# Layer 3 of a four-layer kernel: the first term of y written by VectorE, the first pair's sums beside the second's, stores on ScalarE's queue, and a new step plan

## The chip, the core and the metric

The kernel runs on one NeuronCore of a Trainium2 chip. The core has a matrix engine (TensorE, PE in the profile), VectorE (DVE), ScalarE (ACT), GpSimd (POOL), and a sync engine (SP) that here only issues DMAs. The engines run in parallel, each through its own instructions in order, and wait for one another by semaphores. A PE matmul writes to PSUM, eight banks of 128 x 512 fp32; VectorE and ScalarE read and write PSUM and SBUF; GpSimd works on SBUF. The metric is the device time of one launch in microseconds (us), the median of some runs.

## The reference

A chain of four layers on x of shape (2, 128, 64, 64), fp32. The change is in layer 3, a small Mamba over the channels of each pixel: the 128 channels are 8 tokens of 16 features.

```python
def _mamba(seq, ...):                       # seq: (B*H*W, 8, 16)
    xz = seq @ in_proj_w.T
    xi, z = jnp.split(xz, 2, axis=-1)       # 32 each
    xs = silu(causal depthwise conv of 4 taps over the tokens (xi))
    dt, Bm, Cm = split(xs @ x_proj_w.T)     # 1, 16, 16
    dt = softplus(dt @ dt_proj_w.T + dt_proj_b)
    dA = jnp.exp(dt[..., None] * A)
    dBx = dt[..., None] * Bm[:, :, None, :] * xs[..., None]
    def step(h, inp):
        dA_t, dBx_t, C_t = inp
        h = dA_t * h + dBx_t
        return (h, jnp.einsum('nds,ns->nd', h, C_t))
    ...                                     # scan over the 8 tokens
    y = ys + xs * D
    y = y * silu(z)
    return y @ out_proj_w.T
...
# layer 3: x + silu(groupnorm(mamba(x)))    (4 groups of 32 channels, per image)
```

With h_t = dA_t * h_(t-1) + dBx_t, the sum over states of C_t * h_t falls into two: the sum of C_t * dBx_t, which is (sum over n of B_n * C_n) * dt * xs, and the sum of C_t * dA_t * h_(t-1). The kernel computes the first by itself; it is "the first term of y".

## The kernel before

Layer 3 works on 16 chunks: 2 images x 8 chunks of 512 pixels (`Chunk3`). The channels of a chunk lie on the 128 partitions and the pixels in the free dimension. After the projections, a tile of [128, 2, 512] holds the 8 tokens x 32 inner channels: two halves `i` of four strips of 32 partitions. The scan over 8 tokens is made in four steps `k` of two tokens `o` each; `PLACE[k]` names the half and the strip pair of step k: k = 0 and 1 are the two strip pairs of the first half, k = 2 and 3 those of the second. In the scan, the tiles `A` and `D` have 16 states x 32 channels as 128 partitions x 4 groups, for 512 pixels: [128, 4, 512] for each token.

For each chunk:
- `xs_` and `sz_`: PE projections of x, ScalarE's Silu. `b_`, `c_`: the rows B and C; `b_` copies B by ScalarE into `bs` and stores it to DRAM (`rows`). `dt_`, `e_exp`, `e_ln`, `dt_add`: softplus, with the last add on GpSimd; `dtx_`: dt * xs on GpSimd into `e`; `put` stores dt to DRAM (`ddt`).
- `spread` and `load` bring dt and B back by DMA, spread over the partitions of the scan (`dtr`, `D`). All these DMAs are issued by SP, in order.
- `da_`: ScalarE's Exp makes A. `rx_`: PE spreads dt * xs into PSUM, and `db_` (VectorE) multiplies D by it. `mul` (GpSimd): A = A * h_(t-1), half a token (128 x 1024) at a time. `add` (VectorE, or GpSimd for some): D = D + A, which is the new h. The products and sums of successive tokens are the recurrence; `todo` and `advance` write their order for each step.
- `pc_`: PE spreads C into PSUM (`q`, two buffers); `hc_` (VectorE): A = A * C, a unit `u` of 128 x 1024 at a time; `y_` (PE): sums over the states into a 32-partition strip of the bank `y`.
- `cb_`, `cbx_`, `ecb_`: the first term. `ecb_` writes it into the tile `dt`, half by half; `y1_` adds it to `y` by a matmul with the identity, and `y0_` begins y with D * xs by a matmul with a diagonal matrix.
- `yg_`: y times silu(z) (VectorE). `xr_`: output projection, ScalarE's copy into x. `bn_`: statistics for the group norm. When an image's chunks are done, class `Norm` finishes it: `silu` on ScalarE, `load` of the kept x, `store`: an add on VectorE or GpSimd and the DMA out.

The loop `for s` runs over all (chunk, step) pairs as a pipeline written out by hand. In iteration s, step s-1 is read out (`hc_`, `y_`: `pc_` in the loop), step s does its recurrence (`cc`), step s+1 gets its `db_` and `da_` (`nc_`), and step s+2 its loads (`n2`). Each iteration has four groups `g`; the dictionaries `first` and `extra` hang further work at (k, g), ahead of and behind the group's own, for the chunk in work, the one before (`old`) and the next two (`fut`, `fut2`). Everything is under `tc.manual_schedule()`: each engine runs its instructions in the order of this program.

Lines of the profile: `one` L1165 (PE for `xs_`, `sz_`, `dt_`, `cbx_`), `bc_` L1184, store of `rows` L1193, `cb_` L1200, `dt_add` L1217, `dtx_` L1220, `put` L1224, `spread` L1232, `load` L1244, `ecb_` L1251, `rx_` L1261, `db_` L1265, `da_` L1271, `mul` L1278, `add` L1283, `pc_` L1295, `hc_` L1300, `y0_` L1304, `y1_` L1308, `y_` L1316, `yg_` L1321, `xr_` L1326. PSUM holds one bank each for `misc` and `y`, two for `rx`, and two pairs for `q`. Each call of a matmul on fp32 appears as two records.

Of the kernel before, what the change touches and what calls it, by code (L numbers as in the profile page):

```python
# [7 lines left out]
F32 = mybir.dt.float32  # L8
# [49 lines left out]
def conv_seq_kernel(ctx: ExitStack, tc: tile.TileContext, a: dict, out: bass.AP):  # L58
# [1031 lines left out]
    with ExitStack() as c3:  # L1090
# [61 lines left out]
        class Chunk3:  # L1152
# [4 lines left out]
            def __init__(self, b, ci):  # L1157
                self.b, self.ci = b, ci
                self.sl = slice(ci * T, (ci + 1) * T)
                self.A, self.D, self.rx, self.dtr = {}, {}, {}, {}  # L1160
# [13 lines left out]
            def sz_(self, i):  # L1174
                if i == 0:
                    self.sz = wt("sz", bufs=3)
# [11 lines left out]
            def b_(self):  # L1188
                p = self.bc_(0)
                self.bs = wt("bs", (P, T))  # L1190
                nc.scalar.copy(self.bs, p)
                self.rows = dr.tile([P, T], F32, tag="rows", name="rows")
                nc.sync.dma_start(self.rows, self.bs)  # L1193
# [4 lines left out]
            def cb_(self):  # L1198
                self.cb = wt("cb", (P, T), bufs=1)
                nc.vector.tensor_mul(self.cb, self.bs, self.pc)  # L1200

            def dt_(self, i):
                if i == 0:
                    self.e = wt("e")
                    self.dt = wt("dt")
# [16 lines left out]
            def put(self):  # L1222
                self.ddt = dr.tile([P, 2, T], F32, tag="ddt", name="ddt")
                nc.sync.dma_start(self.ddt, self.dt)  # L1224
# [25 lines left out]
            def ecb_(self, i):  # L1250
                nc.vector.tensor_mul(self.dt[:, i, :], self.e[:, i, :], self.pcb)  # L1251
# [15 lines left out]
            def da_(self, k):  # L1267
                sl = slice(1, 2) if k == 0 else slice(0, 2)
                self.A[k] = wt("A", (P, 2, 4, T), bufs=3)
                for g in range(4):  # L1270
                    act(self.A[k][:, sl, g, :], self.dtr[k][:, sl, :], AF.Exp,  # L1271
                        scale=aneg[:, 2 * NS + g : 2 * NS + g + 1])

            def mul(self, k, o, half):
                g = slice(2 * half, 2 * half + 2)
                h = (self.D[k, 0] if o else self.D[k - 1, 1])[:, g, :]
                a_ = self.A[k][:, o, g, :]
                nc.gpsimd.tensor_mul(a_, a_, h)  # L1278

            def add(self, k, o, half, eng):  # L1280
                g = slice(2 * half, 2 * half + 2)
                d = self.D[k, o][:, g, :]
                eng.tensor_add(d, d, self.A[k][:, o, g, :])  # L1283
# [14 lines left out]
            def hc_(self, k, u):  # L1298
                a_ = self.A[k][:, 1, 2 * u : 2 * u + 2, :] if k == 0 else self.A[k][:, :, u, :]
                nc.vector.tensor_mul(a_, a_, self.q.pop((k, u)))  # L1300

            def y0_(self, i):
                self.y = ps.tile([P, T], F32, tag="y", name="y")
                mm(self.y, lhsT=diag_d, rhs=self.xs[:, i, :], start=True, stop=False,  # L1304
                   skip_group_check=True)

            def y1_(self, i):
                mm(self.y, lhsT=ident, rhs=self.dt[:, i, :], start=False, stop=False,  # L1308
                   skip_group_check=True)

            def y_(self, k, u):
                i, j = PLACE[k]
                last = (1 if k == 0 else 3)
                for o, g in self.unit(k, u):
                    r = slice(32 * (j + o), 32 * (j + o) + 32)
                    mm(self.y[r], lhsT=rep[:, 0:32], rhs=self.A[k][:, o, g, :], start=False,  # L1316
# [355 lines left out]
```

## Time and profile before

| what | us |
|---|---|
| median of 3 runs | 6776.94 (6775.4 to 6785.25) |
| the profiled execution, device time | 6768.67 |
| its span, first to last instruction | 6766.5 |
| layer 3 in it | from 5617 to the end |
| one chunk of layer 3, steady | 65 |

Busy shares over the whole span: PE 88%, DVE 81%, ACT 66%, POOL 80%. They mix four layers; the stages of layer 3 must be read from its own window. In the rows below, "x224" counts instructions, the mean is in ns, and what stands behind the bar is idle time of the engine just before these instructions and what ended it. Layer 3's largest groups on each engine, from 5540 us on:

| line, engine | what | count | mean ns |
|---|---|---|---|
| L1278 POOL | product A * h | 224 | 2358 |
| L1265 DVE | D times rx | 224 | 1212 |
| L1300 DVE | A times C | 224 | 1210 |
| L1283 DVE / POOL | D + A | 128 / 64 | 1720 / 2986 |
| L1295, L1316 PE | C spread, sums into y | 896, 896 | 721, 666 |
| L1271 ACT | Exp of 128 x 1024 | 192 | 1137 |

From 5700 to 6700 us the DMAs moved 158.56 MB, 159 GB/s. By line, KB of an issue and median us to landing: D<-rows 256 KB 6.0, dtr<-ddt 64 KB 2.1, ddt<-dt 512 KB 9.3, rows<-bs 256 KB 2.1, kept<-x 2048 KB 10.9.

### The profile page before, as it was taken

What the parts mean: (1) busy time and instruction counts of PE and PEld (TensorE: products, weight loads), DVE (VectorE), ACT (ScalarE), POOL (GpSimd) and SP (SyncE); (2) the same over time, 40 slices, a digit from 0 to 9 for tenths busy, and PEclk for the clock granted to TensorE, in tenths of its full rate; (3) what the DMA queues carried; (4) which work ended last, traced back from release to release, by engine and by line L of the source; (5) the groups of instructions that cost most, each with busy time, mean ns of one, the idle gap of its engine ahead of it and who ended that gap; (6) DMA issues with size and microseconds to landing.
All of it is one profiled execution on the core that took longest, in us unless ns stands there. A gap on an engine that the chain in (4) does not pass through costs nothing. (4 is left out here: it accounts for less than half of the span.)

```text
span 6766.5 us, 66235 instructions
## 1 busy us (share of the span) xinstructions
PE 5937.2 (88%) x19980; PEld 2785.3 (41%) x19980; DVE 5486.3 (81%) x4456; ACT 4471.8 (66%) x7736; POOL 5390.1 (80%) x2471
## 2 busy tenths in 40 slices
PE   8888888888888888888889999999999997888887
PEld 2222222222222222222248877887788882222221
DVE  7999999999999999999976665665566674777677
ACT  7887788877788777887765654554555564444443
POOL 6999999999999999999976665555566665787676
PEclk7888777877788777887789999999999996898788
DMA  6556666665666656666520000000000004667565
GB/s 185 144 148 159 165 147 146 149 151 143 152 153 155 151 144 152 153 154 150 144 62 1 5 3 1 1 1 1 1 1 1 1 1 107 172 147 164 143 162 124
DMA packets 397882, 700.60 MB, mean 104 GB/s; under 512 B 73801, under 2 KB 76242, under 8 KB 396882
## 3 DMA queue, kind: packets, MB, share of 16 engines
q1 hardware_dynamic: 396640, 694.32, 42.2%
q8 instruction: 157, 2.57, 0.2%
q14 instruction: 203, 1.66, 0.1%
q10 hardware_dynamic: 882, 2.04, 0.1%
HBM read 584.80 MB, written 111.28 MB: 103 GB/s over the span
## 5 line engine op out<-in xcount | busy, mean ns | idle before, releaser
L384 POOL TENSOR_TENSOR dbu<-dus,bs 128x1024 f32<-128x1024 f32 x1024 | 2439.2, 2422 | 114.6 <-DVE h L428 97.6
L428 DVE TENSOR_TENSOR_SCAN h<-da,hst,dbu 128x1024 f32<-128x1024 f32 x896 | 2092.4, 2342 | 86.9 <-ACT dbu L412 83.0
L397 ACT ACTIVATE da<-dts,aneg 128x512 f32<-128x512 f32 (+1 forms) x2048 | 1410.0, 689 | 348.3 <-DVE h L428 310.0
L924 POOL TENSOR_TENSOR sum<-sum,sc 128x1024 f32<-128x1024 f32 x384 | 906.7, 2361 | 491.7 <-ACT sc L919 487.9
L886 ACT COPY sc<-s 128x512 f32<-128x512 f32 x1024 | 597.7, 585 | 859.5 <-PE s L881 745.7
L881 PE MATMUL s<-q,k 128*128 128x256 f32 x4096 | 1052.0, 380 | 7.1 <-DVE k L858 3.5
L893 DVE TENSOR_TENSOR mx<-mx,s 128x512 f32<-128x512 f32 x896 | 610.0, 681 | 546.0 <-ACT sc L886 544.8
L936 PE MATMUL av<-sc,v 128*128 128x256 f32 x4096 | 1049.5, 379 | 2.5 <-ACT sc L919 2.5
L451 PE MATMUL y<-hc,cst 128*32 128x512 f32 x4096 | 875.2, 753 | 192.8 <-DVE hc L440 179.2
L440 DVE TENSOR_TENSOR hc<-h,pc 128x1024 f32<-128x1024 f32 x704 | 843.2, 1198 | 9.7 <-PE y L451 8.1
L881 PEld LDWEIGHTS s<-q,k 128*128 128x128 f32 x4096 | 776.5, 190 | 140.9 <-issue 29.0
L936 PEld LDWEIGHTS av<-sc,v 128*128 128x128 f32 x4096 | 768.8, 190 | 103.2 <-ACT sc L919 3.9
L438 POOL TENSOR_TENSOR hc<-h,cs 128x1024 f32<-128x1024 f32 x320 | 764.8, 2390 | 1.2 <-issue 1.2
L1278 POOL TENSOR_TENSOR A<-A,D 128x1024 f32<-128x1024 f32 x224 | 524.1, 2358 | 230.4 <-DVE D L1283 208.2
L417 PE MATMUL pc<-xd,sel 16*128 16x512 f32 x1024 | 704.5, 778 | 1.4 <-DVE hc L440 1.3
L916 DVE TENSOR_TENSOR sc<-sc,pm 128x1024 f32<-128x1024 f32 x512 | 620.9, 1213 | 0.9 <-PE pm L912 0.9
L919 ACT ACTIVATE sc<-sc 128x1024 f32<-128x1024 f32 x512 | 541.9, 1059 | 8.6 <-DVE sc L916 8.1
L341 PE MATMUL misc<-xd,w_dt 9*128 9x512 f32 x504 | 360.5, 802 | 130.3 <-ACT x L480 69.7
L451 PEld LDWEIGHTS y<-hc,cst 128*32 128x32 f32 x4096 | 125.2, 120 | 846.4 <-DVE hc L440 417.3
L1265 DVE TENSOR_TENSOR D<-D,rx 128x1024 f32<-128x1024 f32 x224 | 269.0, 1212 | 173.0 <-PE q L1295 109.9
L412 ACT ACTIVATE dbu<-hst,dbu,df 128x1 f32<-128x1 f32 x896 | 337.7, 377 | 68.1 <-POOL dbu L384 44.9
L1271 ACT ACTIVATE A<-dtr,aneg 128x1024 f32<-128x1024 f32 (+1 forms) x256 | 245.8, 1031 | 201.5 <-PE y L1316 103.8
(262 smaller groups left out, 7714.0 us busy)
## 6 DMA issues: line engine op xcount, KB each, us to landing
dts<-ddt SPq DMA_DIRECT2D x512, 256.0 KB, 5.5
dus<-ddu SPq DMA_DIRECT2D x512, 256.0 KB, 5.1
D<-rows SPq DMA_DIRECT2D x448, 256.0 KB, 6.0
bs<-rows SPq DMA_DIRECT2D x1024, 64.0 KB, 5.0
cs<-rows SPq DMA_DIRECT2D x1024, 64.0 KB, 3.3
ddt<-dt SPq DMA_DIRECT2D x128, 256.0 KB, 2.0
ddu<-dtu SPq DMA_DIRECT2D x128, 256.0 KB, 4.1
dtr<-ddt SPq DMA_DIRECT2D x448, 64.0 KB, 2.2
```

Source lines behind the costliest of these rows:

```text
L384: nc.gpsimd.tensor_mul(t, self.dus[q], _bc(self.bs[g], 1, [P, 2, T]))
L397: act(t[:, i, sl], self.dts[q][:, i, sl], AF.Exp, scale=an[:, g, 2 * q + i : 2 * q + i + 1])
L417: mm(t, lhsT=sel[32:48, 4 * g : 4 * g + 4, :].rearrange("p n d -> p (n d)"), rhs=self.xd[32:48, :], start=True, stop=True)
L428: nc.vector.tensor_tensor_scan(ho, ai, bi, init, ALU.mult, ALU.add)
L438: nc.gpsimd.tensor_mul(t, self.h[u], _bc(self.cs[gq(u)[0]], 1, [P, 2, T]))
L440: nc.vector.tensor_mul(t, self.h[u], _bc(self.pc[u // 2], 1, [P, 2, T]))
L451: mm(self.y[q // 2][r : r + 32, :], lhsT=sum4, rhs=self.hc[u][:, i, :], start=False, stop=(u % 8 >= 6), skip_group_check=True)
L881: mm(p[:, o, :], lhsT=j.k[m // 8][:, m % 8 * P : m % 8 * P + P], rhs=self.q, start=True, stop=True)
L893: nc.vector.tensor_max(self.mx, self.s[0][:, 0:2, :] if u == 1 else self.mx, self.p[u])
L916: nc.vector.tensor_sub(s, s, _bc(self.pm[:, :], 1, [P, 4, NQ]))
L924: nc.gpsimd.tensor_add(self.sum, self.s[0] if w == 1 else self.sum, self.s[w])
L936: mm(self.av, lhsT=self.job.v[m // 8][:, m % 8, :], rhs=self.s[u // 2][:, m % 4, :], start=(m == 0), stop=(m == 31))
```

## The change

- `ecb_` no longer writes into `dt`: VectorE writes the first term straight into the PSUM bank `y`. `y1_` and its matmuls go. `y` is now one tile for all of layer 3; one matmul with `start=True` writes it once ahead of the loop, and every later matmul into it, `y0_` too, accumulates (`start=False`) on what VectorE wrote.
- The first step's sums (k = 0, one strip, four groups) are no longer made by themselves: `y_` for k = 1 sums the groups of (1, 0), (1, 1) and (0, 1) in turn, into three strips. To hold the first step's A until then it gets a tile of its own, `A0` (one buffer); `A` with its three buffers serves k = 1 to 3.
- The stores of `rows` and of `ddt` are issued by ScalarE in place of SP.
- A table `PLAN` writes out, for each step k and group g, the order of C (`hc_`), D (`db_`), products `m`, adds `v` on VectorE and `g` on GpSimd; "time" is `dt_add` and `dtx_`. It replaces `todo`, `advance` and the order in the loop's body.
- Other work changes place: `sz_` goes from two chunks ahead into the chunk's own steps 1 and 2; `xs_` goes from step 2 to step 1; `dt_` half in step 2, half in step 3; `b_` from the end of step 3 to the start of step 0 of the chunk before; `cbx_` and `ecb_` into the chunk's own steps 1 and 3. Numbers of buffers follow (`sz` 3 to 2, `bs` 2 to 1, `cb` 1 to 2, `e` 2 to 3, `dt` 2 to 1).
- x is kept in four DMAs of 1024 pixels in place of one; the group norm's loads, adds and stores are made in eight pieces of 512 pixels in place of four of 1024, and its small operations are hung elsewhere. For the second image `silu` stays at 1024.

```diff
             def b_(self):
                 p = self.bc_(0)
-                self.bs = wt("bs", (P, T))
+                self.bs = wt("bs", (P, T), bufs=1)
                 nc.scalar.copy(self.bs, p)
                 self.rows = dr.tile([P, T], F32, tag="rows", name="rows")
-                nc.sync.dma_start(self.rows, self.bs)
+                nc.scalar.dma_start(self.rows, self.bs)
...
             def put(self):
                 self.ddt = dr.tile([P, 2, T], F32, tag="ddt", name="ddt")
-                nc.sync.dma_start(self.ddt, self.dt)
+                nc.scalar.dma_start(self.ddt, self.dt)
...
             def ecb_(self, i):
-                nc.vector.tensor_mul(self.dt[:, i, :], self.e[:, i, :], self.pcb)
+                nc.vector.tensor_mul(y, self.e[:, i, :], self.pcb)
...
             def da_(self, k):
+                t = wt("A0", (P, 1, 4, T), bufs=1) if k == 0 else wt("A", (P, 2, 4, T), bufs=3)
                 sl = slice(1, 2) if k == 0 else slice(0, 2)
-                self.A[k] = wt("A", (P, 2, 4, T), bufs=3)
...
             def y0_(self, i):
-                self.y = ps.tile([P, T], F32, tag="y", name="y")
-                mm(self.y, lhsT=diag_d, rhs=self.xs[:, i, :], start=True, stop=False,
+                mm(y, lhsT=diag_d, rhs=self.xs[:, i, :], start=False, stop=False,
                    skip_group_check=True)
 
-            def y1_(self, i):
-                mm(self.y, lhsT=ident, rhs=self.dt[:, i, :], start=False, stop=False,
-                   skip_group_check=True)
-
             def y_(self, k, u):
-                i, j = PLACE[k]
-                last = (1 if k == 0 else 3)
-                for o, g in self.unit(k, u):
-                    r = slice(32 * (j + o), 32 * (j + o) + 32)
-                    mm(self.y[r], lhsT=rep[:, 0:32], rhs=self.A[k][:, o, g, :], start=False,
-                       stop=(u == last and k % 2 == 1), skip_group_check=True)
+                for kk, o in ((k, 0), (k, 1), (0, 1))[: 3 if k == 1 else 2]:
+                    r = 32 * (PLACE[kk][1] + o)
+                    mm(y[r : r + 32], lhsT=rep[:, 0:32], rhs=self.A[kk, o][:, u, :],
+                       start=False, stop=False, skip_group_check=True)
...
+        PLAN = (
+            ("m10 m11 C D", "C D time", "C v10 D", "g11 D C"),
+            ("m00 m01 C D v00", "C v01 D m10 m11", "v10 D", "g11 D"),
+            ("m00 m01 C D v00", "C v01 m10 m11", "C v10 D", "g11 C"),
+            ("m00 m01 C D", "C v00 D g01 m10 m11", "C D", "D C"),
+        )
+        y = ps.tile([P, T], F32, tag="y", name="y")
+
         with tc.manual_schedule():
+            mm(y, lhsT=ident, rhs=x[:, 0, 0:T], start=True, stop=True)
             c, c1 = chunks[:2]
             for i in range(2):
                 c.xs_(i)
-            for i in range(2):
-                c.sz_(i)
             c.b_()
...
             for i in range(2):
-                c.cbx_(i)
-                c.ecb_(i)
-            for i in range(2):
                 c1.xs_(i)
-            for i in range(2):
-                c1.sz_(i)
+            c1.dt_(0)
...
-                if cc is not None:
-                    more((1, 1), lambda: cc.y0_(0), at=first)
-                    more((1, 3), lambda: cc.y1_(0), at=first)
-                    more((3, 1), lambda: cc.y0_(1), lambda: cc.y1_(1), at=first)
-                    more((3, 0), lambda: cc.yg_(0))
+                if fut is not None:
+                    more((0, 0), fut.b_, at=first)
+                    more((0, 1), fut.c_, at=first)
+                    more((0, 2), fut.put, fut.cb_)
                 if old is not None:
                     more((1, 0), lambda: old.yg_(1))
-                    more((1, 2), old.xr_)
-                    more((2, 0), old.bn_)
+                    more((2, 1), old.xr_, at=first)
+                    more((2, 3), old.bn_)
+                if cc is not None:
+                    more((1, 0), lambda: cc.cbx_(0), at=first)
+                    more((1, 0), lambda: cc.ecb_(0))
+                    more((1, 3), lambda: cc.y0_(0), at=first)
+                    more((1, 3), lambda: cc.sz_(0), at=first)
+                    more((2, 0), lambda: cc.sz_(1), at=first)
+                    more((3, 0), lambda: cc.cbx_(1), at=first)
+                    more((3, 0), lambda: cc.yg_(0), lambda: cc.ecb_(1))
+                    more((3, 3), lambda: cc.y0_(1), at=first)
                 if fut2 is not None and s >= 0:
-                    more((2, 0), lambda: fut2.xs_(0))
-                    more((2, 1), lambda: fut2.xs_(1))
-                    more((2, 2), lambda: fut2.sz_(0))
-                    more((2, 3), lambda: fut2.sz_(1))
+                    more((1, 1), lambda: fut2.xs_(0), at=first)
+                    more((1, 2), lambda: fut2.xs_(1), at=first)
+                    more((2, 3), lambda: fut2.dt_(0), at=first)
                 if fut2 is not None:
-                    more((3, 1), lambda: fut2.dt_(0))
-                    more((3, 2), lambda: fut2.dt_(1), fut2.e_exp, fut2.e_ln)
-                    more((3, 3), fut2.b_)
-                if fut is not None:
-                    more((0, 0), fut.c_, fut.dt_add, fut.dtx_)
-                    more((0, 1), fut.cb_)
-                    more((0, 2), lambda: fut.cbx_(0))
-                    more((0, 3), fut.put)
-                    more((1, 0), lambda: fut.ecb_(0), lambda: fut.cbx_(1))
-                    more((1, 1), lambda: fut.ecb_(1))
+                    more((3, 2), lambda: fut2.dt_(1), fut2.e_exp, fut2.e_ln, at=first)
                 if 0 <= ci < B:
-                    more((1, 3), lambda: nc.sync.dma_start(kept[ci], x[:, ci, :]))
+                    sl = slice(1024 * k, 1024 * k + 1024)
+                    more((k, 3), lambda: nc.sync.dma_start(kept[ci][:, sl], x[:, ci, sl]))
...
                 if ci == NCH + 1:
-                    more((2, 3), *[lambda j=j: nrm.silu(j) for j in range(4)])
-                    more((0, 0), lambda: nrm.load(0), lambda: nrm.load(1))
-                    more((2, 4), lambda: nrm.store(0, G), lambda: nrm.load(2))
-                    more((3, 2), lambda: nrm.store(1, V), lambda: nrm.load(3))
-                    more((3, 4), lambda: nrm.store(2, G), lambda: nrm.store(3, V))
...
+                    more((0, 1), nrm.fourth)
+                    more((1, 2), *[lambda j=j: nrm.silu(j) for j in range(4)])
+                    more((1, 2), lambda: nrm.load(0))
+                    for j in range(8):
+                        at_ = (2 + j // 4, j % 4)
+                        if j < 7:
+                            more(at_, lambda j=j: nrm.load(j + 1))
+                        more(at_, lambda j=j: nrm.store(j, (G, V)[j % 2]))
...
                 for g in range(4):
-                    if g < units:
+                    ops = PLAN[k][g].split()
...
+                    if "C" in ops:
                         prepare()
+                    if pc_ is not None and pk and g:
+                        pc_.y_(pk, g - 1)
+                    (older, ok) = at(s - 2)
                     if g == 0 and older is not None and ok:
                         older.y_(ok, 3)
                     for f_ in first.get((k, g), []):
                         f_()
```

After these, the new loop issues `da_` in group 0, then the plan's operations in their order, then what hangs at `extra`.

## The prediction, made before the change was run

> **What bounds the kernel now.** Layer 3 is the last part of the span, from 5617 us to 6766.5 us, and the change touches nothing else, so I read only there. First the page's rows for the loop. Columns: line, engine, operation, tiles, shapes, count | busy us, mean ns | idle before, and its releaser.
>
> ```profile
> L1278 POOL TENSOR_TENSOR A<-A,D 128x1024 f32<-128x1024 f32 x224 | 524.1, 2358 | 230.4 <-DVE D L1283 208.2
> L1265 DVE TENSOR_TENSOR D<-D,rx 128x1024 f32<-128x1024 f32 x224 | 269.0, 1212 | 173.0 <-PE q L1295 109.9
> ```
>
> GpSimd stands idle for VectorE's add and VectorE for TensorE: the two engines of the recurrence wait in turn. Next the busy time by stretch, for one steady chunk (us, then PE, PEld, DVE, ACT, POOL busy with counts, clock, DMA share, GB/s):
>
> ```profile
> 6070.00:6135.00 65.00, 54.34 (x164) 14.08 (x162) 49.39 (x43) 28.70 (x33) 50.17 (x21) 0.89 0.65 154
> ```
>
> No engine is full: of 65 us PE idles about 11, DVE 15.6, POOL 15. So a chunk is bound by the order of waits, not by an engine. The list of waits, 5600 to 6600 us, then the same list for SP's queue (total us, times, longest):
>
> ```profile
> POOL A L1278 <- DVE D L1283: 187.1, 58, 10.3
> ...
> DVE D L1265 <- PE q L1295: 101.5, 26, 6.4
> ...
> PE misc L1165 <- DVE dt L1251: 76.8, 16, 7.6
> ...
> DVE dt L1251 <- DMA ddt<-dt: 47.2, 14, 7.0
> ```
> ```profile
> SPq L1193 <- ACT bs L1191: 288.0, 15, 23.1
> ```
>
> Last the timeline of one chunk (start, us, engine, line, tiles, [idle before <- releaser]), which joins them:
>
> ```profile
> 6095.97 0.69 DVE L1251 TENSOR_TENSOR dt<-e,misc 128x512 f32<-128x512 f32 x1 [3.14 <-DMA ddt<-dt]
> 6096.72 2.08 PE L1165 MATMUL misc<-cb,nsum 128*128 128x512 f32 x2 [5.07 <-DVE dt L1251]
> 6102.74 3.29 PE L1316 MATMUL y<-A,cst 128*32 128x512 f32 x4
> 6111.72 1.22 DVE L1265 TENSOR_TENSOR D<-D,rx 128x1024 f32<-128x1024 f32 x1 [5.89 <-PE q L1295]
> ```
>
> `ecb_` overwrites dt while the store of dt is still read, so VectorE stands 3.14 us; the second `cbx_` waits for it, so PE stands 5.07 us and comes back at half speed (2.08 us against 1.12 for the same pair at 6084.47); behind it come the first pair's sums (3.29 us), `xr_` and `y1_`; VectorE's next product waits 5.89 us for rx. That is 9 us of VectorE in each chunk.
>
> **The floor.** What must the recurrence keep? An add on VectorE (L1283) takes 1.22 us when GpSimd is idle, else this:
>
> ```profile
> 5985.82 1.88 DVE L1283 TENSOR_TENSOR D<-D,A 128x1024 f32<-128x1024 f32 x1
> 5984.26 2.36 POOL L1278 TENSOR_TENSOR A<-A,D 128x1024 f32<-128x1024 f32 x1 [3.96 <-DVE D L1283]
> ```
>
> It ends at 5987.70, 1.08 us after GpSimd's operation ends (5986.62): it ran only then. The GpSimd add issued at 5972.47 behind such an add takes 3.22 us instead of 2.37. So I count those two kinds as excluding each other: per chunk 20 GpSimd operations (14 products, 4 adds, dt_add, dtx) x 2.36 = 47.2, and 8 VectorE adds x 1.09 = 8.7, together **55.9 us**. The other VectorE products read PSUM and do not wait.
>
> **How near the floor?** The trace has an example: the last chunk, with no next chunk to prepare (no dt store, `ecb_`, dt_add, dtx). From 6679.18 to 6732.39 (`y0_(1)` to `y0_(1)`) it takes 53.2 us, with 18 GpSimd operations: floor 18 x 2.36 + 8.7 = 51.2, so 2.0 us are lost. 55.9 + 2.0 = **57.9 us** a chunk is my period, against (6701.98 - 5706.4 - 26.8) / 15 = 64.6 now (26.8 is the group norm's extra, below).
>
> **Part by part.**
> - *First term into y's bank.* Goes: `y1_`, 2 calls a chunk, 1.77 + 1.02 us in this chunk's PE; the wait on the dt store with what follows it (9 us of VectorE). Comes: VectorE writes PSUM, which no row shows. Below, 0.59 us (the spacing of L1251, same operands); above, twice 0.68; nearest is L1251 itself, so 0. New order: `ecb_` comes after `yg_` on VectorE, and `y0_` and the sums come after it on PE. Late next is the second `ecb_`, step 3: it needs PE's last sum of the first half and `cbx_(1)` (about 1.0 + 1.1 us) while VectorE has one product each of C and D (2.3 us) and `yg_` (0.6) to do, so at most about 1 us; inside the 2.0.
> - *First pair's sums beside the second's.* Now they run alone: 3.29 + 1.90 us. A pair in two column strips takes 1.05. A third strip costs between 0 and 0.95 us each, four times: PE gains 5.2 down to 1.4. Nearest is the pair's row: 5.2. With `y1_` PE falls from 54.3 to about 46 us; it isn't on the path unless its order is.
> - *Stores by ScalarE's queue.* SP no longer stands 288/15 = 19 us a chunk before L1193. The Trainium skill (DMA: Bandwidth & Descriptors, "Issuing engines are not separate DMA queues") speaks against a gain: all queues run on the same 16 engines, and only issue time is saved. The row agrees in part: the dt store lands in 9.3 us (median of the steady part), behind the loads. By the rule I leave it at 9.3; by the row of free stores (rows<-bs, 2.1) it would be 7.2 shorter; either way 0 on the path, since dt is overwritten half a chunk later and spread two steps later. ScalarE now waits in `put` for dt_add, and the Exp of the step after is queued behind; dt_add comes third on GpSimd (2 x 2.36 + 2.36 = 7.1 us into the step), that Exp a step (14 us) later: 0. Without cover it would be a few us a chunk. Two issues of 0.34 us on ScalarE, 28.7 of 65 busy, are hidden. SP's remaining waits are for the D and dtr buffers, as before.
> - *Loads as a bound?* 10 MB a chunk; 5700 to 5800 us moved 206 GB/s at share 0.80, which is 49 us a chunk: below 57.9.
> - *New order of adds, A0.* VectorE's adds stand earlier in its queue, so GpSimd's 187 us of waits shrink; Exp no longer waits for y's sums (69.8 us in that list, ScalarE, off the path). Both are in the period. Projections move a step; ScalarE's table loads stay at about 4 a chunk (62 x 1.28 us over 16 chunks now).
> - *Head.* Two z projections leave the serial start: 5632.40 to 5637.97, 5.6 us; the second chunk's (4.8) leave too but the loads arrive then (5674.98) and a dt projection comes: between 5.6 and 10.4 with the wait for `ecb_`; I take **6**.
> - *Group norm of image 0.* Now chunks 9 and 10 take 82.5 and 74.2 us, 26.8 over twice 65: adds of 1024 at 2.87 us, SP behind stores. In halves the port work stays (4 GpSimd adds of 512 at 1.27 and 4 of VectorE, about 0.6 each: 7.5 us) and four Silu (4.6 us) still stand before a projection. Extra between 7.5 and 26.8; I take 14, as port plus Silu is 12: gain **13**. Four stores of x in place of one of 2 MB: 0, chunks 0 and 1 already bear it.
> - *Tail.* The last add and store are halves: **1**.
>
> Sum: 15 x (64.6 - 57.9) = 100.5, + 6 + 13 + 1 = **120.5 us**. Against the profiled execution (6768.67, span 6766.5) 6648; the median shown is 8.3 above that execution, so 6776.94 - 120.5 = 6656. I say **6655 us**, 1.8% less.
>
> **The rule that speaks against it.** SBUF — State Buffer, "Who interferes with whom": a VectorE instruction with two SBUF inputs and a GpSimd one that reads SBUF exclude each other, and the second waits for the whole of the first. A denser GpSimd makes this dearer. By the row (mean 1720 ns of L1283) VectorE sums to 28 x 1.13 + 6 x 0.6 + 8 x 1.72 = 49.0 us; by the rule with GpSimd never idle 8 x 3.45 gives 62.8, which would be the period. Laid out step by step, an add that GpSimd itself waits for pays least and one that falls behind a product pays up to 3.35 (the longest in the trace); I get a mean near 2.4, so 54.4: just under the floor. That is what I am least sure of.
>
> **Rivals.**
> 1. *The floor is reached* (55.9): for it, the new order hands GpSimd two products before each wait; against, PE still drops to half speed after gaps of 2.3 us. 15 x 8.7 + 20 = 150: 6627. Chance 0.18.
> 2. *VectorE becomes the bound by the port* (61 to 63): the rule above; 62.8 gives 15 x 1.8 + 20 = 47: 6730; at 61, 6703. Chance 0.19.
> 3. *Slower: adds wait fully and VectorE also waits for PE.* Each add at 3.45 and PE's order (one misc bank and one y bank, `ecb_` in front of the sums) leaving the waits of step 3 (2.80 + 1.74 us before L1300 and L1265 now): 62.8 + 4.5 = 67.3, so 15 x 2.7 - 20 = +20: 6797. It decides once VectorE's work and waits pass 64.6 + 20/15 = 65.9. Against: PE loses 8 us of work. Chance 0.05.
> 4. *The dt wait was hidden anyway* and the period stays about 64.6; then only the 20 us of head, norm and tail are left: 6757. Against: the waits above follow each other on one chain. Chance 0.03.
>
> Forecast (57 to 60 us a chunk): 0.55. The range: 6610 (floor and a better norm) to 6715 (60.5 and little from the norm). Less than 0.2% (13.5 us) can't be told from no change; faster 0.92 (forecast, rivals 1 and 2), same 0.02 (most of rival 4), slower 0.06 (rival 3, and 0.01 for the rest).
>
> **What would show it.** Chunks 57 to 60 us apart; no wait for ddt<-dt before the first term; POOL busy near 50 of 58; L1283 on VectorE near 2.4 us; DVE's wait for PE q under 2 us a chunk; PE busy about 46; SP never held by bs. Wrong would be: VectorE without idle time at more than 61, or ScalarE standing in `put` with GpSimd waiting for A.

## The result, and the profile after

The kernel after the change takes 6696.0 us (median of 4 runs, 6684.2 to 6706.7) against 6779.9 us for the kernel before on the same chip: ratio 0.9876, 95% interval 0.9856 to 0.9895, or 84 us less. The prediction was 6655 with a range of 6610 to 6715.

The profiled execution took 6684.23 us (span 6682.4). VectorE's last reciprocal of layer 2 begins at 5627.45 us there and at 5617.44 in the kernel before, so layers 0 to 2, whose code is the same, took 10.0 us longer in this execution. Counted from there, layer 3 fell from 1149.1 to 1054.9 us, by 94.2. Chunks are counted below from one `cb_` on VectorE to the next; "period" is the mean of the eleven intervals that hold neither the start nor the group norm. It fell from 65.7 to 60.9 us. The prediction said 57.9, within 57 to 60.

First the page's rows for the two sides of the recurrence (busy us, mean ns | idle before, and its releaser):

```profile
L1283 POOL TENSOR_TENSOR A<-A,D 128x1024 f32<-128x1024 f32 x224 | 526.8, 2370 | 194.1 <-DVE D L1288 146.4
...
L1266 DVE TENSOR_TENSOR D<-D,rx 128x1024 f32<-128x1024 f32 x224 | 268.6, 1211 | 143.9 <-DMA D<-rows 120.3
```

VectorE's product waits mainly for a load now (120.3 us), no longer for TensorE's q (109.9 before). The windows row of one chunk (60 us: PE, PEld, DVE, ACT, POOL busy, clock, DMA share, GB/s) still has no full engine:

```profile
6000.00:6060.00 60.00, 49.25 (x156) 12.90 (x154) 52.26 (x42) 28.64 (x32) 48.11 (x20) 0.89 0.71 164
```

The list of waits of the engines, then that of SP's queue, both from 5650 to 6560 us (total us, times, longest):

```profile
POOL A L1283 <- DVE D L1288: 126.5, 45, 8.6
...
DVE D L1266 <- DMA D<-rows: 114.5, 21, 16.8
...
DVE D L1266 <- PE q L1300: 15.1, 14, 1.9
```
```profile
SPq L1232 <- DMA rows<-bs: 213.0, 13, 20.7
```

The last line is the surprise. `spread` (L1232) reads `ddt`, not `rows`, yet SP stands 213 us for the store of `rows` to land. The timeline of one chunk shows what follows from it:

```profile
5991.51 0.58 ACT L1191 COPY bs<-misc 128x512 f32<-128x512 f32 x1 [5.00 <-PE misc L1184]
...
5992.12 0.33 ACTq L1193 DMA_DIRECT2D rows<-bs  x1
...
5994.09 0.33 ACTq L1224 DMA_DIRECT2D ddt<-dt  x1
...
5994.20 5.48 SPq L1232 DMA_DIRECT2D dtr<-ddt  x8
...
5999.80 3.91 SPq L1244 DMA_DIRECT2D D<-rows  x8
...
6001.47 4.26 ACT L1273 ACTIVATE A<-dtr,aneg 128x1024 f32<-128x1024 f32 x4 [3.12 <-DMA dtr<-ddt]
...
6007.80 1.22 DVE L1266 TENSOR_TENSOR D<-D,rx 128x1024 f32<-128x1024 f32 x1 [6.09 <-DMA D<-rows]
...
6010.23 2.35 POOL L1283 TENSOR_TENSOR A<-A,D 128x1024 f32<-128x1024 f32 x1 [6.78 <-DVE D L1288]
```

SP issues nothing from about 5975.7 us on until 5994.20, when `rows` has just landed (5994.14); after two spreads it stops once more, until `ddt` has landed (5997.04). Its loads of D go at 5999.80, 8.3 us after the copy of bs, and VectorE and GpSimd each stand 6 to 7 us for them. The list of instructions of the compiled kernel tells why: its DMAs, whichever engine issues them, use eight completion semaphores in turn, and each waits until the DMA that used its semaphore before, eight places ahead, has landed. The list gives the places in the order of the program, not of time: six of SP's loads, issued by 5975.4 us, and the store of `ddt` stand between the store of `rows` and the first spread of step 0, although ScalarE issues that store only at 5992.12. So the first spread stands eight places behind the store of `rows`, the third eight behind the store of `ddt`. The Trainium skill (DMA: Bandwidth & Descriptors, "Why a DMA increments its semaphore by 16 and not by 1") says what that wait guards against: with two DMAs in flight on one semaphore, a count can be reached before the first has landed (no run here shows that).

### The profile page after: what moved, and what is told of

Same layout as the page of the kernel before. It is cut to its first block, busy times and chain, and to the rows that moved or that the text cites. A ratio compares the mean times of both kernels' runs of the same rounds, so it can differ in the third digit from the quotient of the medians.

```text
span 6682.4 us, 66184 instructions
## 1 busy us (share of the span) xinstructions
PE 5857.7 (88%) x19918; PEld 2766.3 (41%) x19918; DVE 5536.6 (83%) x4462; ACT 4477.6 (67%) x7740; POOL 5404.5 (81%) x2473
## 5 line engine op out<-in xcount | busy, mean ns | idle before, releaser
L1266 DVE TENSOR_TENSOR D<-D,rx 128x1024 f32<-128x1024 f32 x224 | 268.6, 1211 | 143.9 <-DMA D<-rows 120.3
L1300 PE MATMUL q<-xs,lc 32*128 32x512 f32 x896 | 301.0, 678 | 64.9 <-DVE A L1306 63.9
```

## The experiments

All are runs on one core, each beside the kernel before, whose median was 6774.2 to 6779.9 us in these groups of runs; the ratios are what to compare. "Bs to D" is the median time from the copy of bs to SP's next issue of D loads in the trace; it is left out where the order of the two differs.

| kernel | median us | ratio to before, interval | period us | bs to D us |
|---|---|---|---|---|
| before | 6779.9 | 1 | 65.7 | |
| after | 6696.0 | 0.9876 (0.9856 to 0.9895) | 60.9 | 8.29 |
| late2 | 6689.5 | 0.9864 (0.9847 to 0.9881) | 60.8 | 8.08 |
| early | 6630.7 | 0.9780 (0.9766 to 0.9795) | 57.0 | |
| sp_store | 6641.6 | 0.9796 (0.9781 to 0.9811) | 56.7 | 4.79 |
| rows_sp | 6686.8 | 0.9864 (0.9847 to 0.9881) | 61.0 | 8.58 |
| ddt_sp | 6658.2 | 0.9827 (0.9804 to 0.9850) | 58.8 | 5.85 |
| before_act | 6948.4 | 1.0254 (1.0231 to 1.0277) | 77.2 | |
| before_t1 | 6710.2 | 0.9899 (0.9880 to 0.9918) | 60.6 | |
| term_by_pe | 6679.5 | 0.9854 (0.9838 to 0.9871) | 60.5 | |
| old_order_sp | 6689.1 | 0.9864 (0.9849 to 0.9879) | 60.3 | |
| first_pair_sp | 6639.4 | 0.9793 (0.9780 to 0.9807) | 57.1 | |
| term_by_pe_sp | 6621.6 | 0.9768 (0.9754 to 0.9781) | 56.0 | |
| early_ddt_sp | 6632.7 | 0.9787 (0.9770 to 0.9804) | 56.4 | |

### What holds the loads

The theory from the trace was that ScalarE's two stores hold SP; the rivals were buffers in use, a full DMA, or VectorE and GpSimd at their limit. **early** computes and stores B two steps earlier and issues the store of dt a step later:

```diff
-                    more((0, 0), fut.b_, at=first)
                     more((0, 1), fut.c_, at=first)
-                    more((0, 2), fut.put, fut.cb_)
+                    more((0, 2), fut.cb_)
+                    more((1, 0), fut.put)
...
+                    more((2, 2), fut2.b_, at=first)
...
+                    if s < 0:
+                        more((3, 3), fut2.b_, at=first)
```

> Changed against the kernel after: B of a chunk is computed and stored two steps earlier (step 2 of the chunk two before), and the store of dt is issued at the start of step 1 instead of in step 0; the loads stay in their places. Theory 1 (ScalarE's stores hold SP's loads by the ring of eight): SP issues the loads of step 0 some 10 to 15 us earlier, the wait of the D product for D<-rows falls from 114 us to below 40, the chunk period from 60.8 to 56 to 58 us, layer 3 from 1055 to 985 to 1010, time 6625 to 6655. Rival A (buffers) and rival B (bandwidth): the wait for D<-rows stays above 90 us, layer 3 within 15 us of 1055. Rival C (VectorE and GpSimd are the bound by their shared port): the wait for D<-rows goes but the period falls by 1.5 us at most, layer 3 1030 to 1055.

Measured: 6630.7 us, layer 3 1003.3 us, period 57.0. The list of waits of early:

```profile
DVE D L1266 <- DMA D<-rows: 34.6, 6, 16.0
```

What is left of the wait for loads lies at the start, six times between 5670 and 5754 us (in the kernel after 114.5 us, 21 times), with the same buffers and the same bytes. Rivals A and B fall; C too, since the period fell by 3.9. This run moves the projection of B on TensorE as well; sp_store below moves nothing but the issuer.

**late2** leaves everything in place but issues the store of `rows` later, just ahead of the store of dt.

```diff
+            def keep_rows(self):
                 self.rows = dr.tile([P, T], F32, tag="rows", name="rows")
                 nc.scalar.dma_start(self.rows, self.bs)
...
-                    more((0, 2), fut.put, fut.cb_)
+                    more((0, 2), fut.keep_rows, fut.put, fut.cb_)
```

> Changed against the kernel after: the store of rows is issued by ScalarE later in step 0 (just ahead of the store of dt, behind the Exp of that step); nothing else. Theory 1 (a DMA waits until the one eight issues before it has landed, so SP's loads of step 0 are held by ScalarE's two stores whoever issues them): SP is held 3 to 6 us a chunk longer, the wait of VectorE's D product for D<-rows grows from 114 us to 160 or more, layer 3 takes 30 to 90 us more than the 1055 us of the kernel after, time about 6725 to 6785. Rival A (the loads are late because their D and dtr buffers are still in use) and rival B (the DMA engines are full): no load waits for the store, so layer 3 stays within 10 us of 1055.

Measured: 6689.5 us, period 60.8: no change, which is what rivals A and B had said. The timeline of late2 shows that the edit did not do what the expectation took for granted:

```profile
5987.92 0.59 ACT L1191 COPY bs<-misc 128x512 f32<-128x512 f32 x1 [5.00 <-PE misc L1184]
...
5989.83 0.33 ACTq L1195 DMA_DIRECT2D rows<-bs  x1
...
5990.19 0.44 ACTq L1226 DMA_DIRECT2D ddt<-dt  x1
...
5995.89 4.04 SPq L1246 DMA_DIRECT2D D<-rows  x8
```

The store went only 1.3 us later than in the kernel after (1.91 us behind the copy instead of 0.61), because it did not fall behind all of the step's Exp; and the store of dt, 2.27 us behind the copy against 2.58, is the last to land in both. SP is released at the same time. The run tells nothing between the theories.

**sp_store** gives both stores back to SP, in the same places of the program.

```diff
-                nc.scalar.dma_start(self.rows, self.bs)
+                nc.sync.dma_start(self.rows, self.bs)
...
-                nc.scalar.dma_start(self.ddt, self.dt)
+                nc.sync.dma_start(self.ddt, self.dt)
```

> Changed against the kernel after: both stores (rows and dt) are issued by SP again, in the same places of the program; nothing else. Theory 1 (SP is held by the landing of the stores when ScalarE issues them, and by their data when SP does): the move gave nothing, layer 3 within 15 us of 1055, time 6680 to 6710. The prediction's view (on ScalarE's queue the stores leave SP free, so SP's 19 us a chunk are gained for the loads): undoing it costs 2 to 6 us a chunk, layer 3 1085 to 1145, time 6725 to 6785.

Measured: 6641.6 us, 54 us less than after (the intervals of the two ratios are apart), period 56.7. Both expectations were wrong, and the theory was incomplete: it had SP held as long either way. The timeline of sp_store:

```profile
5969.51 0.59 ACT L1191 COPY bs<-misc 128x512 f32<-128x512 f32 x1 [5.00 <-PE misc L1184]
...
5970.12 0.34 SPq L1193 DMA_DIRECT2D rows<-bs  x1
...
5970.51 3.68 SPq L1232 DMA_DIRECT2D dtr<-ddt  x8
...
5974.30 3.69 SPq L1244 DMA_DIRECT2D D<-rows  x8
...
5976.03 4.27 ACT L1273 ACTIVATE A<-dtr,aneg 128x1024 f32<-128x1024 f32 x4 [0.35 <-DMA dtr<-ddt]
```

SP stands for bs as long as ever (its list has 218.4 us for that). But it goes on as soon as the store is issued: the first spread follows in 0.39 us, and all eight go in 3.68 us instead of 5.48. From the copy to the D loads it is 4.79 us, not 8.29. The rule of eight places holds on SP's own queue too. The eighth spread behind the store of `rows` goes at 5973.77 us, when that store has landed (5972.20), so it need not wait. The store of dt, issued by SP after the D loads, does hold:

```profile
5978.08 0.46 SPq L1224 DMA_DIRECT2D ddt<-dt  x1
...
5979.10 8.48 SPq L1232 DMA_DIRECT2D dtr<-ddt  x8
```

These eight spreads are drawn out to 8.48 us, each standing eight places behind a DMA still under way: the second goes at 5980.22, when the third load of D has landed (5980.20), the last at 5987.28, when the store of dt has (5987.26). So what counts is not how long SP stands, but which DMA stands eight places behind a store: the next that SP has to issue, as with ScalarE's stores, or one that comes after seven others, as with SP's.

This was put to the test by giving SP one store only: in **rows_sp** the first line pair of the last diff, in **ddt_sp** the second.

> Changed against the kernel after: the store of rows alone is issued by SP again; the store of dt stays with ScalarE. Theory 1, made finer by the run with both stores on SP (a store that ScalarE issues holds SP's DMA eight places behind it until it has landed; one that SP issues holds nobody, SP goes on as soon as it is issued): here the second load of step 0 still stands eight behind the store of dt and waits until that has landed (at 5997.06 in the kernel after, the last of the two), so little is won: period 59.8 to 61.2 us (60.9 in the kernel after), time 6675 to 6705. Rival D (the cost lies with ScalarE: its issues and its standing for dt_add delay its Exp): one store less to issue wins about half of the 4.2 us: period 58.3 to 59.3.

> Changed against the kernel after: the store of dt alone is issued by SP again; the store of rows stays with ScalarE. Theory 1: SP's first load of step 0 waits for the landing of rows (5994.20 in the kernel after), but the third no longer for that of dt (5997.06), so the loads of the step end some 2.9 us earlier: period 57.3 to 59 us, time 6640 to 6670. Rival D (ScalarE's own time): about half of 4.2 us, 58.3 to 59.3; the two differ by the run with the store of rows alone on SP, which by theory 1 wins next to nothing and by rival D as much as this one.

Measured: rows_sp 61.0 us a chunk and 6686.8, ddt_sp 58.8 us and 6658.2. VectorE's wait for the loads of D in rows_sp, ddt_sp and sp_store (114.5 us in the kernel after):

```profile
DVE D L1266 <- DMA D<-rows: 108.7, 19, 16.2
```
```profile
DVE D L1266 <- DMA D<-rows: 93.3, 25, 16.0
```
```profile
DVE D L1266 <- DMA D<-rows: 68.0, 25, 16.8
```

That a store issued by SP holds nobody, as the expectations have it, goes too far, as sp_store shows; their forecast rests only on the DMAs next in SP's order. While the store of dt, which lands last, is with ScalarE, moving that of `rows` brings nothing; moving that of dt brings half of the 4.2 us. Over the five kernels the table's two last columns rise together: 4.79, 5.85, 8.08, 8.29 and 8.58 us from bs to D go with periods of 56.7, 58.8, 60.8, 60.9 and 61.0. Rival D, which wanted the same gain from each, is out.

**before_act** makes the opposite test: the kernel before with only its two stores moved to ScalarE (the same lines, `nc.sync` to `nc.scalar`).

> Changed against the kernel before, one thing: both stores are issued by ScalarE instead of SP. Theory 1 (a store on ScalarE's queue holds SP's later loads until it has landed): no gain, 0 to 3 us a chunk slower, time 6775 to 6825. The prediction's view (SP stands 19 us a chunk for bs, and is freed): the loads go earlier, same or up to 2 us a chunk faster, time 6745 to 6777.

Measured: 6948.4 us, 2.5% slower than before. The sign is that of theory 1, the size is not: 11.5 us a chunk instead of 0 to 3. In before_act's waits (SP's queue, then the engines) the held DMAs are the D loads themselves:

```profile
SPq L1244 <- DMA rows<-bs: 255.5, 10, 27.0
```
```profile
DVE D L1265 <- DMA D<-rows: 130.3, 13, 17.0
```

Why a place in the ring that falls on other loads costs that much more was not followed further.

### What the wait for the store of dt was worth

**before_t1** is the kernel before with one cause of waiting taken away: the first term goes to a tile of its own, not over dt. TensorE's matmul with the identity stays; to make room, dt and bs have one buffer each.

```diff
-                self.bs = wt("bs", (P, T))
+                self.bs = wt("bs", (P, T), bufs=1)
...
-                    self.dt = wt("dt")
+                    self.dt = wt("dt", bufs=1)
...
-                nc.vector.tensor_mul(self.dt[:, i, :], self.e[:, i, :], self.pcb)
+                if i == 0:
+                    self.t1 = wt("t1")
+                nc.vector.tensor_mul(self.t1[:, i, :], self.e[:, i, :], self.pcb)
...
-                mm(self.y, lhsT=ident, rhs=self.dt[:, i, :], start=False, stop=False,
+                mm(self.y, lhsT=ident, rhs=self.t1[:, i, :], start=False, stop=False,
```

> Changed against the kernel before, one thing: ecb_ writes the first term into a tile of its own instead of over dt (dt and bs get one buffer, to make room), so it no longer waits for the store of dt; the matmul with the identity stays, as do all orders. Theory P (the prediction: 3.1 us of VectorE's wait and the 5.9 us behind it sit on one chain): the period falls by 3 to 6 us from 65.7, to 60 to 63, time 6690 to 6735. Rival 4 of the prediction (the wait is hidden anyway, or the next wait takes its place): period 64.5 to 65.7, time 6755 to 6777.

Measured: 6710.2 us, period 60.6. The list of waits of before_t1, whose lines answer to the first three shown of the kernel before:

```profile
POOL A L1280 <- DVE D L1285: 101.2, 54, 10.8
...
DVE D L1267 <- PE q L1297: 47.5, 22, 6.3
...
PE misc L1165 <- DVE t L1253: 33.3, 16, 5.4
```

In the same stretch of the kernel before (5650 to 6560 us) they are 174.6, 96.0 and 71.1 us: the first falls to about three fifths, the other two to half. This one wait was worth 5.0 us a chunk and about 64 us in all, as much as three quarters of what the whole change brought.

### The other parts, one by one

**term_by_pe** is the kernel after with the first term in an SBUF tile of its own and TensorE's matmul with the identity; **term_by_pe_sp** is the same with both stores by SP, where no late load can hide it.

```diff
-                nc.vector.tensor_mul(y, self.e[:, i, :], self.pcb)
+                self.t1 = wt("t1", (P, T), bufs=1)
+                nc.vector.tensor_mul(self.t1, self.e[:, i, :], self.pcb)
...
-                mm(y, lhsT=diag_d, rhs=self.xs[:, i, :], start=False, stop=False,
+                mm(y, lhsT=diag_d, rhs=self.xs[:, i, :], start=True, stop=False,
...
+            def y1_(self):
+                mm(y, lhsT=ident, rhs=self.t1, start=False, stop=False, skip_group_check=True)
...
-                    more((1, 3), lambda: cc.y0_(0), at=first)
+                    more((1, 3), lambda: cc.y0_(0), cc.y1_, at=first)
...
-                    more((3, 0), lambda: cc.yg_(0), lambda: cc.ecb_(1))
-                    more((3, 3), lambda: cc.y0_(1), at=first)
+                    more((3, 0), lambda: cc.yg_(0), lambda: cc.y0_(1), lambda: cc.ecb_(1))
+                    more((3, 1), cc.y1_, at=first)
```

> Changed against the kernel after: VectorE writes the first term into an SBUF tile of its own (not dt, so nothing waits for the store of dt), and PE adds it to y by the identity matmul as before the change. PE has 2 calls a chunk more (1.8 + 1.0 us) and the order on PE needs them ahead of the sums. Theory 1 (the first-term edit gained mainly the wait on the store of dt; the matmuls were beside other work): layer 3 within 15 us of 1055. Rival (PE's work and order count, PE misc and y banks being in the chain): 1 to 4 us a chunk more, layer 3 1070 to 1115.

> Changed against the kernel after: both stores by SP (as sp_store, 56.7 us), and the first term goes into an SBUF tile of its own and is added to y by PE (2 calls, about 2.8 us a chunk), as in term_by_pe. Theory H: hidden here too, period 56.2 to 57.7 us, time 6630 to 6655. Rival (it was hidden in term_by_pe only because the loads were late there): 58 to 60.5 us, time 6660 to 6700.

Measured: 6679.5 against 6696.0 with the intervals overlapping, and 6621.6 against 6641.6 for sp_store, with the intervals meeting at 0.9781. The two matmuls are hidden, and writing the bank y by VectorE gains nothing over a free tile; it rather loses, 0.7 us a chunk by the periods. Why is not settled: VectorE's product waits 10.3 us for q in term_by_pe_sp and 23.8 in sp_store, but the chunk intervals of sp_store also swing from one to the next (54.6 to 59.3 us), and those of term_by_pe_sp (55.6 to 56.7 us) do not.

**first_pair_sp**, with both stores by SP, makes the first pair's sums alone again:

```diff
-                for kk, o in ((k, 0), (k, 1), (0, 1))[: 3 if k == 1 else 2]:
+                for kk, o in ((k, 0), (k, 1)):
...
+            def y0k(self, u):
+                for g in (2 * u, 2 * u + 1):
+                    mm(y[32:64], lhsT=rep[:, 0:32], rhs=self.A[0, 1][:, g, :],
+                       start=False, stop=False, skip_group_check=True)
...
+                    if pc_ is not None and pk == 0 and g > 1:
+                        pc_.y0k(g - 2)
```

> Changed against the kernel after: both stores by SP (as sp_store, 56.7 us), and the sums of the first pair are made alone again, two matmuls in each half of step 1, instead of beside the second pair's. PE has about 3.8 us more a chunk. Theory H (PE is not on the path, its 49 us of 57 leave room): period 56.2 to 57.7 us, time 6630 to 6655. Rival (PE's order is on the path through q and misc): 58 to 60.5 us, time 6660 to 6700.

Measured: 6639.4 us, period 57.1. TensorE's saving is worth nothing that can be measured.

**old_order_sp**, with both stores by SP, has the order of products and adds of the kernel before in the new table:

```diff
-            ("m10 m11 C D", "C D time", "C v10 D", "g11 D C"),
-            ("m00 m01 C D v00", "C v01 D m10 m11", "v10 D", "g11 D"),
-            ("m00 m01 C D v00", "C v01 m10 m11", "C v10 D", "g11 C"),
-            ("m00 m01 C D", "C v00 D g01 m10 m11", "C D", "D C"),
+            ("C D m10 m11 v10 time", "C D g11", "C D", "D C"),
+            ("C D m00 m01 v00", "C D v01", "D m10 m11 v10", "D g11"),
+            ("C D m00 m01 v00", "C v01", "C D m10 m11 v10", "C g11"),
+            ("C D m00 m01 v00", "C D g01 m10 m11", "C D", "D C"),
```

> Changed against the kernel after: both stores are issued by SP (as in the run sp_store, period 56.7 us, where no load is late), and the table PLAN gives the products, adds, C and D of each step in the order that the kernel before had. Theory O (the order of the adds and products itself is worth time once loads and the wait for the store of dt are out of the way): GpSimd waits longer for VectorE's adds, period 58 to 61 us, time 6660 to 6705. Rival (the two waits were all; any sensible order reaches the same): period 56.2 to 57.5, time 6630 to 6655.

Measured: 6689.1 us, period 60.3. The order is worth 3.6 us a chunk. The waits of old_order_sp show both sides of it: VectorE now stands for GpSimd too, which it did not in sp_store.

```profile
POOL A L1283 <- DVE D L1288: 105.4, 47, 6.3
...
DVE D L1288 <- POOL A L1283: 14.1, 18, 2.3
```

### Is VectorE the next bound?

**early_ddt_sp** is early with the store of dt by SP, so that it holds no load.

> Changed against the kernel early (B stored two steps earlier by ScalarE, store of dt at the start of step 1; period 57.05 us): the store of dt is issued by SP, so that it no longer holds SP's loads until it lands (102 us of SP's waits there). Theory V (the loads are no longer what bounds; VectorE was busy 56.1 of 57 us there, with its adds lengthened to more than 2 us beside GpSimd): period 56.3 to 57.3 us, time 6615 to 6640. Rival (late loads still cost some of it): period 55 to 56.2 us, time 6590 to 6615.

Measured: 6632.7 us, period 56.4: no faster than early (6630.7), as theory V had it. The windows rows from 5800 to 6100 us of the kernel after and of early_ddt_sp, and then the groups of VectorE's add (L1288) in the same two, from 5650 to 6560 us:

```profile
5800.00:6100.00 300.00, 253.84 (x772) 65.24 (x768) 259.03 (x205) 139.24 (x156) 242.25 (x98) 0.85 0.71 167
```
```profile
5800.00:6100.00 300.00, 263.81 (x848) 67.40 (x842) 291.31 (x227) 152.79 (x170) 265.06 (x108) 0.94 0.77 183
```
```profile
L1288 DVE TENSOR_TENSOR D<-D,A 128x1024 f32<-128x1024 f32 x113 | 246.5, 2182 | 0.1
```
```profile
L1288 DVE TENSOR_TENSOR D<-D,A 128x1024 f32<-128x1024 f32 x121 | 286.5, 2368 | 5.7 <-POOL A L1283 5.1
```

VectorE is busy 291 of 300 us, 97%, where the kernel after had 86%: it is the bound there, though part of that busy time is its adds standing beside GpSimd's operations (mean 2.37 us against 1.70 in the same stretch of the kernel before). The shortest mean period of all kernels is 56.0 us. It is met by term_by_pe_sp (VectorE busy 276 of the same 300 us), which at 6621.6 us is 1.1% faster than the kernel after and 2.3% faster than the kernel before. Its form of the first term was not tried together with early's order.

## Why the prediction was right, and where it was not

The sign was right, the time lay in the range, and an order of waits was what bound the kernel. The period was not right: 60.9 us, outside the 57 to 60 of the forecast and close to the 61 of rival 2, whose cause it does not have, since VectorE stood idle for loads. The range was wide enough to hold a loss on the stores that the prediction did not foresee; that much is luck. By the prediction's own parts:

- **What bounds the kernel**: an order of waits with the wait for the store of dt at its head. Shown by before_t1: 5.0 us a chunk from that wait alone. Of the 9 us of VectorE that the prediction put on it, no more than that showed in the period. In the kernel after, the first term waits for no store.
- **First term into y's bank**: VectorE's write to PSUM takes 0.696 us (0.684 into SBUF before), as taken. The gain came from leaving dt alone, not from the bank (term_by_pe, term_by_pe_sp).
- **First pair's sums**: three calls (six records) in three strips take 1.06 us in the trace, two calls in two strips 1.05, so the third strip is free, as taken. It brings no time (first_pair_sp). TensorE fell to about 50 us a chunk (49.25 of 60 us), not 46; its x projection (L1165 from x and lm) got dearer, 1.14 us a record against 0.72, after its waits for VectorE's `ecb_`.
- **Stores by ScalarE's queue**: the step that failed, put at no cost: "SP no longer stands 288/15 = 19 us a chunk before L1193" and "SP's remaining waits are for the D and dtr buffers, as before", with 0 on the path either way. SP stands for the landing of the same stores instead, and that costs 4.2 us a chunk and 54 us in all (sp_store against after). The rule of the Trainium skill that the prediction cites there (DMA: Bandwidth & Descriptors, "Issuing engines are not separate DMA queues"), that all queues run on the same 16 engines, was weighed for the wrong quantity: it bears on the transfers, and here a shared set of completion semaphores decided. By that rule the prediction also left the store of dt at 9.3 us to its landing; in the chunk shown it lands in 2.95 us, with no load of SP's in flight. Where loads are in flight, as in early, ScalarE's store takes 7.8 us (median), which agrees with the rule.
- **New order**: taken into the period without a size of its own; 3.6 us a chunk (old_order_sp).
- **The rule that speaks against**, VectorE's adds beside GpSimd: the mean rose from 1.70 to 2.18 us, near 2.4 as taken, and 2.37 where no load was late. The sum just under the floor stood: VectorE is the bound at 56.4 us a chunk, not at the 61 to 63 of rival 2.
- **The floor** of 55.9 us: no mean period went below it. The period of 57.9 was reached as soon as SP issued the stores (56.7).

The account: predicted 113.5 us from the chunks with the group norm, of which 82.3 came (982.9 to 900.7 us from first to last `cb_`; the norm's share in it 12.4, predicted 13); head 5.5 (6); tail 6.3 (1). In the last read-out TensorE runs at half clock for some 20 us in the kernel before and some 6 in the kernel after (last section shows such a difference between kernels with the same code there), so the gain of the tail is not shown to come from the change. Together that makes the 94.2 us of layer 3, less the 10.0 us by which the unchanged layers differ between the two profiled executions.

In parts, by the periods: 65.7, less 5.0 for the wait on dt, less 0.4 for all else in old_order_sp, less 3.6 for the order, plus 4.2 for the stores on ScalarE, is 60.9. This is a chain of kernels (before, before_t1, old_order_sp, sp_store, after), so the sum closes by itself, and taken in another order the parts differ: the same move of the stores cost 11.5 us in the kernel before.

## What to carry to other kernels

Before a DMA is moved to another queue, ask which later DMAs wait for it to land. Where completion semaphores are shared in turn, a store on another engine's queue takes its place among loads that go long before it, and so can hold the very next load; on the load's own queue, the DMAs between are issued after it, and it has more time to land. In the list of waits such a hold shows as a DMA waiting for a transfer whose data it does not read. And when a change of many parts gains, undo and do its parts one at a time: here one untied buffer was worth as much as three quarters of the gain, one part gave 54 us back, and two brought nothing.

## What the runs showed that was not expected

The end of layer 3 takes 125 to 129 us from the last `cb_` in most profiled executions of the kernel after and its variants, 138 in old_order_sp and 144 in two (sp_store, late2), though late2 runs the same instructions there as the kernel after. The difference of these two is TensorE's clock in the last read-out. Windows rows at the same places of that read-out, of the kernel after and then of late2 (the clock is the third number from the end):

```profile
6646.00:6650.00 4.00, 4.00 (x10) 0.70 (x8) 1.10 (x2) 0.00 (x0) 3.92 (x3) 0.50 0.00 0
...
6658.00:6662.00 4.00, 4.00 (x17) 0.84 (x16) 1.98 (x2) 0.00 (x0) 0.43 (x1) 1.00 0.00 0
```
```profile
6646.00:6650.00 4.00, 4.00 (x10) 1.01 (x6) 1.34 (x3) 0.00 (x0) 3.92 (x2) 0.50 0.00 0
...
6658.00:6662.00 4.00, 4.00 (x10) 0.69 (x6) 1.22 (x1) 0.00 (x0) 0.00 (x0) 0.50 0.00 0
```

Both drop to half after TensorE's idle time of about 2.5 us; the kernel after is back at full speed some 6 us later, late2 stays at half for about 30 us, although TensorE is busy throughout; sp_store does the same. The Trainium skill (TensorE: Matmul & The Clock Gate, "Part 1: The HAM clock gate") gives about 3.4 us of sustained work for the way back; late2's trace does not agree. Why it stays is open. This is one reason why single profiles of this kernel differ by some 17 us (the unchanged layers differ too), and why the parts above are compared by their periods as well as by their medians.
